# Pacing the side work of a gather-driven kernel: one generator counts more of its steps, two others get other stretches

## The chip, the cores and the metric

The kernel runs on one core of a Trainium2 chip. The metric is the device time of one execution in microseconds (us), from launch to the end of the last instruction. A core has five engines that run side by side, each in the order its instructions were written: TensorE (PE in the profile, PEld for its weight loads), VectorE (DVE), ScalarE (ACT), GpSimd (POOL) and SyncE (SP), which here only issues DMAs.

## What is computed

Four layers with residuals on four images of 256 channels and 64 x 64 pixels, all in float32. Each layer first normalizes its input over groups of channels (`_gn`).

```python
x = x + deformable(_gn(x))   # 1x1 conv, 3x3 depthwise -> offsets and masks, bilinear sampling
                             # at 9 points in 4 groups, projection, squeeze-excite, feed-forward
x = x + linear(_gn(x))       # qkv (1x1), 5x5 depthwise of q, k, v, linear attention, projection
x = x + binary(_gn(x))       # 3x3 convolution with binarized weights
x = x + pooled(_gn(x))       # attention of 4096 pixels over 1024 max-pooled ones, projection
...
# linear: per group of 8 channels, over (qkv, its depthwise convolution)
vk = einsum('bhdn,bhen->bhde', v, k)
out = einsum('bhde,bhen->bhdn', vk, q) / (einsum('bhe,bhen->bhn', k.sum(-1), q) + EPS)
```

## The kernel before

The work is written by Python generators. Each is one piece of one layer for one image, writes a few instructions and yields a cost, a number that stands for the time of what it has just written. A sampling of one image (`sample`) sets the beat: it has 16 blocks of 18 rounds, 288 rounds in all. A round issues four indirect gathers on POOL (L596), of 128 rows each, into one of seven buffers `g`, and then 16 small matmuls (L603) that weigh and add the rows into the accumulator `acc`. Every two rounds ACT copies the accumulator (`at`, L608), PE turns it (`dp`, L613) and ACT copies it on (`dT`, L623). Every 18 rounds PE projects the block (`po`, L636), and the result goes to memory as `x2`.

`beside(steps, number, *works)` writes the other generators in between. Each work has a total cost and a stretch from `lo` to `hi`, as shares of the sampling. After each round a work writes steps as long as what it has spent is below its total times its share of the stretch. Whatever is left when `hi` is reached is written at once. PE, DVE, ACT and POOL keep the written order (`manual_schedule`), so the pacing is the order of each engine's queue.

Beside sampling n run, for n from 1 on: feed-forward of image n-1 (`feed`, matmuls L739 and L749, cost 328), linear attention of image n-1 (`linear`), and, for n of 2 and 3, convolution and pooled attention of image n-2 in one generator (`second`, cost 568; matmuls L1085, then L1142, then per tile L1185, L1197, L1203). Sampling 0 has the first convolutions of the next images beside it. After sampling 3 the rest is written without a sampling: image 3's feed-forward, its linear attention with image 2's `second`, then image 3's `second`. There `self.alone` is true.

Linear attention makes its rows of q, k, v with matmuls (L821), pads them and runs 24 depthwise chains of 25 taps on DVE (L178, in `depthwise`); after three taps it calls `step(3.9)`. `step` takes one item from the list `later`, if there is one, and runs it. The last third of the chains are those of q. After each pair of them (there are four) `output` puts its work into `later` by way of `staged`, as 15 items: denominators (L921) and their reciprocal (L926), twice four heads (`rden`, L934, and `ot`, L938) and twice two projections (L943) with their relu (L947) and sum (L951). The items of one output are taken during the next pair; those of the last output when the chains are over, in the loop `while later` at the end of `layer1`. An item taken in a step adds nothing to the cost that the step yields.

Of the kernel before, what the change touches and what calls it, by code (L numbers as in the profile page):

```python
# [38 lines left out]

CONVOLVE, OFFSETS, BINARY = NB * 9 + 26, 60, 62  # L40
FEED = NB * 40 + 8
LINEAR, LAST = 938, 624
STEPS = 900
CONV, SECOND = NB * 22.5 + 11, 568
EPS_BN = 1e-5
EPS_GN = 1e-5
# [25 lines left out]
class Net:  # L72
# [684 lines left out]
    def layer1(self, n, st, st2):  # L757
# [3 lines left out]
        with tc.tile_pool(name=f"la{n}", bufs=1, side="right") as sp, \  # L761
# [13 lines left out]
            later, count, aside = [], 0, None  # L775
            alone = self.alone
            room = lambda bufs, more=1: bufs + more * alone

            def step(cost, chains=False):


                nonlocal count
                count += chains
                if later and (not alone or count % 2 or not chains):
                    later.pop(0)()
                if chains:
                    if count % 8 == 6 if alone else count in LEADS:
                        next(made, None)
                    if count % 2 and aside:
                        next(aside, None)  # L790
                return cost
# [3 lines left out]
            def staged(items):  # L795


                for i in range(len(items) + max(map(len, items)) - 1):
                    now = [it[i - k] for k, it in enumerate(items) if 0 <= i - k < len(it)]
                    later.append(lambda now=now: [f() for f in now])  # L800

            sums = self.ps1.tile([P, 2, 2, P], F32, name="vk", tag="vk")
            ks = [sp.tile([P, 2, NB], F32, name=f"ks{t}") for t in range(2)]
# [38 lines left out]
            def aggregate(pd, i, name, done, relu=True, **more):  # L842

                acc = self.ps1.tile([P, 16, W], F32, name="agg", tag="agg")
                out = bp.tile([P, 16, W], F32, name=name, tag="ag", bufs=3)
                yield from self.depthwise(acc, pd, self.w5[:, i], 5, 16, W, 0, bias=self.b5[:, i:i + 1],
                                          step=lambda cost: step(cost, True), out=out)
                end(out, done, relu, **more)
# [12 lines left out]
            def outer(t, kind, kv, vv, first, last):  # L861
# [28 lines left out]
                if alone:  # L890
                    staged([(partial(turned, cs), partial(copied, i), partial(added, i)) for i, cs in enumerate(at)])
                else:
                    later.extend(partial(both, i) for i in range(len(at) + 1))
# [16 lines left out]
            def output(c, qp, aq):  # L910
# [48 lines left out]
                if alone:  # L959
                    order = [heads[0, j] for j in range(4)] + [heads[1, 0], outs[0, 0], heads[1, 1], outs[0, 1], heads[1, 2], heads[1, 3]]  # L960
                    staged([(dens, inverse), none, none] + order + [none, outs[1, 0], outs[1, 1]])
                else:
                    joined = lambda *fs: [f() for f in fs]
                    items = [(partial(joined, dens, inverse),), none]
                    for h in range(2):
                        items += [(partial(joined, *heads[h, j]),) for j in range(4)]
                        items += [(partial(joined, *outs[h, m][:2]), outs[h, m][2]) for m in range(KT)]
                    staged(items)
# [25 lines left out]
            if alone:  # L994
                for _ in range(8):
                    next(made)
                    yield step(0.5)
                    yield step(0.5)
# [22 lines left out]
                    yield from aggregate(*args, **more)  # L1021
                    number += 1
            while later:
                yield step(2 if alone else 4)


    def layer2(self, n, st, st3, side="left"):
# [190 lines left out]
    def run(self):  # L1218
        self.setup()
        tile = lambda name, shape: self.cp.tile(shape, F32, name=name)  # L1220
        ssum = [tile(f"ssum{n}", [P, KT, NBLK]) for n in range(N)]
        st = {i: [tile(f"st{i}{n}", [P, KT, NB, 6]) for n in range(2)] for i in (1, 2, 3)}

        feed = lambda n: self.feedforward(n, ssum[n], st[1][n % 2])
        linear = lambda n: self.layer1(n, st[1][n % 2], st[2][n % 2])

        conv = lambda n, side="left": self.layer2(n, st[2][n % 2], st[3][n % 2], side)
        pooled = lambda n, wide=False: self.layer3(n, st[3][n % 2], wide)

        def second(n):  # L1230
            yield from conv(n)
            yield from pooled(n)

        def beside(steps, number, *works):


            spent, open_ = [0] * len(works), set(range(len(works)))

            def advance(share):
                for j in sorted(open_):  # L1240
                    work, total, lo, hi = works[j]
                    while j in open_ and lo <= share and spent[j] < total * (share - lo) / (hi - lo) or share >= hi:
                        cost = next(work, None)
                        if cost is None:
                            open_.discard(j)
                        if not cost:
                            break
                        spent[j] += cost

            for i, _ in enumerate(steps, 1):  # L1250
                advance(i / number)
            while any(works[j][3] <= 1 for j in open_):
                advance(1)

        rounds = NBLK * BR
        E = mybir.EngineType
        ordered = lambda: self.tc.manual_schedule(engines={E.PE, E.DVE, E.Activation, E.Pool})
        behind = lambda n: [(feed(n), FEED, 0, 0.2), (linear(n), LINEAR, 0.2, 1)]
        with self.tc.tile_pool(name="gather", bufs=2, side="left") as self.gp, \
                self.tc.tile_pool(name="samp", bufs=2, side="left") as self.sp:  # L1260
            with self.tc.tile_pool(name="pw", bufs=1, side="right") as wp, \
                    self.tc.tile_pool(name="pa", bufs=1, side="right") as sp, \
                    self.tc.tile_pool(name="pb", bufs=2, side="right") as bp:
                w = self.weights(wp)

                pads, used = [], []  # L1270
                convolved = (y for i in range(1, N) for y in self.convolve(i, w, sp, bp, pads, used))
                shifted = lambda first, last: (self.shifts(first, last, w["mw"], bp, pads, used), (last - first) * OFFSETS)
                beside(range(64), 64, (self.convolve(0, w, sp, bp, pads, used), CONVOLVE, 0, 1), (*shifted(0, 1), 0.3, 1))
                with ordered():
                    beside(self.sample(0, ssum[0]), rounds, (convolved, (N - 1) * CONVOLVE, 0, 0.96), (*shifted(1, N * NCH), 0, 1))
            with ordered():
                beside(self.sample(1, ssum[1]), rounds, (self.binarise(), BINARY, 0, 0.2), *behind(0))
                for n in range(2, N):
                    beside(self.sample(n, ssum[n]), rounds, *behind(n - 1), (second(n - 2), SECOND, 0.2, 0.9))
        self.idle, self.alone, self.spare = cycle(["acc", "dp"]), True, True  # L1280
        rest = second(N - 2)
        with ordered():
            beside(range(STEPS), STEPS, (feed(N - 1), FEED, 0, 0.27), (linear(N - 1), LAST, 0.27, 1), (rest, SECOND, 0.27, 1.05))
        self.spare = False
        beside(range(STEPS), STEPS, (conv(N - 1, "right"), CONV, 0, 1), (rest, 150, 0, 1))

        self.banks = cycle(["mm", "mm", "mm", "vk"])
        for _ in pooled(N - 1, True):
            pass
# [94 lines left out]
```

## Time and profile before

| | |
|---|---|
| median of 3 runs | 7713.78 us (7711.9 to 7732.44) |
| the profiled execution | 8695.07 us, span 8693.3 us, mean granted TensorE clock 0.803 |
| gathers of sampling 0, first to last | 137 to 1908 us |
| sampling 1 | 1909 to 3615 us |
| sampling 2 | 3616 to 5405 us |
| sampling 3 | 5405 to 7191 us |
| first matmul L739 of image 3's feed-forward | 7234 us |

The profile comes from one execution under the profiler, which takes longer than the others; all durations and waits are from it. A group of instructions is named by its line, engine and operation, then output tile and input tiles. After the bar stand its busy time in us, the mean of one in ns, and the idle time of its engine just before it, with what ended that idle time. "Remote" is an event whose source the profile does not tell.

### The profile page before, as it was taken

Reading aid. Unit: us, or ns where it says so; the run is one execution under the profiler, and the core shown is the slowest. Engines: PE = TensorE matmul, PEld = TensorE weight load, DVE = VectorE, ACT = ScalarE, POOL = GpSimd, SP = SyncE. Lnnn points to the kernel's source line nnn. Section 1 sums busy time; section 2 is a strip of 40 time slices with the busy share of each in tenths; the row PEclk is TensorE's granted clock in tenths of the full one; section 3 lists DMA queues with packets and bytes.
Section 4 is the critical chain, followed back from the end, with each engine's and each line's share of the span. In section 5 each row is a group of like instructions: output and inputs, shape, how many; then the busy total and the mean of one; then the engine's idle time right before and its main releaser. Section 6 shows DMA issues by size and latency. Waiting matters only on the chain.

```text
span 8693.3 us, 99761 instructions
## 1 busy us (share of the span) xinstructions
PE 5880.0 (68%) x35776; PEld 3498.6 (40%) x35776; DVE 4817.7 (55%) x6045; ACT 3541.0 (41%) x10767; POOL 4934.7 (57%) x4870
## 2 busy tenths in 40 slices
PE   4454554448744446688876676888766778986899
PEld 2232222224323222234644443345544333664476
DVE  5344442443366667324776675228766762699833
ACT  2333333234444433334445443444454442456414
POOL 2666666466666666666666556666655560476410
PEclk7676766669866667799988887999878879998899
DMA  6454554444533334444543344445433342220131
GB/s 172 129 160 123 145 149 118 114 143 148 158 107 106 110 109 126 137 127 138 142 133 111 111 116 138 146 135 142 141 105 111 112 118 96 74 72 29 44 97 54
DMA packets 744383, 1031.75 MB, mean 119 GB/s; under 512 B 354128, under 2 KB 459984, under 8 KB 742352
## 3 DMA queue, kind: packets, MB, share of 16 engines
q0 software_dynamic: 221184, 604.27, 24.4%
q1 hardware_dynamic: 522704, 421.10, 16.4%
q8 instruction: 283, 4.64, 0.2%
q14 instruction: 212, 1.74, 0.1%
HBM read 856.39 MB, written 168.61 MB: 118 GB/s over the span
## 4 chain that ended last, share of the span: by engine, by line
PE 43%; another core or an unknown queue 17%; DVE 17%; ACT 13%; issue 8%; DMA 1%; POOL 0%; SPq 0%; ACTq 0%; DVEq 0%; POOLq 0%
DVE agg L178 10%; PE acc L603 6%; PE ps L739 5%; PE ps L749 5%; ACT wm L588 5%; PE ps L1085 4%; PE ps L821 3%; PE ps L943 2%; PE ps L1203 2%; PE s L1185 2%; PE po L636 2%; ACT dT L623 2%; ACT at L608 1%; PE rden L934 1%
## 5 line engine op out<-in xcount | busy, mean ns | idle before, releaser
L596 POOL DMA_INDIRECT g<-tab,sl x4608 | 4399.0, 955 | 2790.8 <-issue 1179.7
L178 DVE SCALAR_TENSOR_TENSOR agg<-pad,vec,agg 128x1024 f32<-128x1024 f32 x2280 | 2934.5, 1287 | 63.9
L603 PE MATMUL acc<-g,wm 128*32 128x128 f32 x18432 | 1012.4, 336 | 2022.6 <-ACT at L608 1471.8
L603 PEld LDWEIGHTS acc<-g,wm 128*32 128x32 f32 x18432 | 557.7, 129 | 2524.7 <-ACT at L608 1683.4
L588 ACT ACTIVATE wm<-sl,con 128x48 f32<-128x48 f32 x6144 | 1490.1, 366 | 26.0 <-remote 12.6
L1085 PE MATMUL ps<-xd,w 128*128 128x256 f32 x3072 | 741.0, 392 | 37.6 <-issue 30.1
L623 ACT COPY dT<-dp 64x128 f32<-64x128 f32 x1152 | 297.2, 258 | 985.8 <-remote 524.3
L1085 PEld LDWEIGHTS ps<-xd,w 128*128 128x128 f32 x3072 | 587.3, 196 | 159.0 <-issue 79.0
L739 PE MATMUL ps<-x2f,f 128*128 128x512 f32 x1024 | 502.3, 639 | 10.2 <-issue 5.1
L608 ACT COPY at<-acc 128x256 f32<-128x256 f32 x576 | 214.5, 372 | 712.8 <-remote 607.4
L821 PE MATMUL ps<-xr,qw 128*128 128x512 f32 x768 | 463.5, 733 | 21.8 <-issue 8.5
L724 DVE SCALAR_TENSOR_TENSOR hm<-ps,vec,lk 128x512 f32<-128x512 f32 x256 | 190.6, 750 | 502.4 <-ACT lk L741 375.2
L749 PE MATMUL ps<-hm,f 128*128 128x512 f32 x1024 | 463.6, 601 | 0.0
L741 ACT ACTIVATE lk<-ps,low 128x512 f32<-128x512 f32 x256 | 174.0, 687 | 514.7 <-PE ps L739 413.2
L636 PE MATMUL po<-dT,ow 128*128 128x288 f32 x1024 | 336.7, 477 | 56.5 <-issue 13.8
L875 ACT COPY kt<-pt 128x512 f32<-128x512 f32 x256 | 149.5, 585 | 544.8 <-remote 246.8
L1036 POOL TENSOR_TENSOR xd<-xp 128x640 f32<-128x640 f32 x64 | 79.8, 1275 | 497.3 <-DMA xq<-x 280.3
L1203 PE MATMUL ps<-gt,pT 128*128 128x129 f32 x2048 | 316.5, 315 | 47.1 <-ACT pT L1199 32.9
L613 PE MATMUL dp<-ident,at 128*128 128x128 f32 x1152 | 285.5, 336 | 77.1 <-ACT dT L623 53.4
L1203 PEld LDWEIGHTS ps<-gt,pT 128*128 128x128 f32 x2048 | 297.2, 226 | 98.8 <-ACT pT L1199 45.0
L1185 PE MATMUL s<-ph,th 128*128 128x512 f32 x512 | 289.2, 677 | 42.9 <-DVE ot L938 9.2
L739 PEld LDWEIGHTS ps<-x2f,f 128*128 128x128 f32 x1024 | 199.2, 203 | 253.3 <-issue 238.5
(243 smaller groups left out, 7710.6 us busy)
## 6 DMA issues: line engine op xcount, KB each, us to landing
g<-tab,sl POOLq DMA_INDIRECT x4608
x<-x SPq DMA_DIRECT2D x128, 512.0 KB
xr<-x SPq DMA_DIRECT2D x96, 512.0 KB
tab<-xo SPq DMA_DIRECT2D x192, 128.0 KB
x<-in_x SPq DMA_DIRECT2D x32, 512.0 KB
y<-yc SPq DMA_DIRECT2D x32, 512.0 KB
yb<-y SPq DMA_DIRECT2D x64, 256.0 KB
x<-yb SPq DMA_DIRECT2D x64, 256.0 KB
```

What stands on the lines that cost most here:

```text
L178: nc.vector.scalar_tensor_tensor(to, s, wt, acc, ALU.mult, ALU.add)
L588: nc.scalar.activation(wm[:, :, :, o], blocks[b][:, r:r + WR, G:], AF.Copy, scale=self.con("own")[:, o:o + 1])
L596: nc.gpsimd.indirect_dma_start(out=g[:, i, :], out_offset=None, in_=table, in_offset=bass.IndirectOffsetOnAxis(ap=sl.bitcast(I32)[:, r, i: ...
L603: nc.tensor.matmul(acc[32 * i:32 * i + 32, :], wm[:, r4, 4 * i + 2 * x:4 * i + 2 * x + 2, :], g[:, i, x * P:(x + 1) * P], start=x == 0, st ...
L623: nc.scalar.copy(dT[b][hs, :, r:r + UR], dp[u][hs, :, :, s, :].rearrange("p v g o -> p g v o"))
L636: nc.tensor.matmul(po[m][:, 0:BR * OB], self.ow[:, k, m * P:(m + 1) * P], dT[b][:, k].rearrange("p r o -> p (r o)"), start=k == 0, stop=k ...
L739: nc.tensor.matmul(ps, f1[:, k, m * P:(m + 1) * P], x2[:, k], start=k == 0, stop=k == KT - 1)
L749: nc.tensor.matmul(ps, f2[:, k, m * P:(m + 1) * P], hm[:, k], start=k == 0, stop=k == 4 * KT - 1)
L821: nc.tensor.matmul(ps, qw[:, k, m * P:(m + 1) * P], x[:, k], start=k == 0, stop=k == KT - 1)
L1085: nc.tensor.matmul(ps[:, e], w[:, k, t, 2 * half + e, m * P:(m + 1) * P], v[:, 2 * half + e, k, t:t + 8], start=i % 6 == 0, stop=i % 6 == 5)
L1185: nc.tensor.matmul(s[i], tv[:, 4 * b + j], ph[:, i * 512:(i + 1) * 512], start=True, stop=True)
L1203: nc.tensor.matmul(ps[:, 0:P + 1], pT[:, m], gt[:, m], start=m == 0, stop=m == 7)
```

## The change

Items that `staged` puts into `later` carry a cost of 1.1, and `step` adds it to what it yields when it has taken such an item, unless linear attention runs without a sampling. In the closing loop a step costs 1 instead of 4 beside a sampling. The total `LINEAR` becomes 956. Feed-forward runs over 0 to 0.22 of a sampling instead of 0 to 0.2, linear attention over 0.22 to 1 instead of 0.2 to 1, and convolution with pooled attention over 0.22 to 1 instead of 0.2 to 0.9.

```diff
-LINEAR, LAST = 938, 624
-STEPS = 900
+LINEAR, LAST = 956, 624
+STEPS, BEGUN = 900, 0.22
...
                 if later and (not alone or count % 2 or not chains):
-                    later.pop(0)()
+                    todo = later.pop(0)
+                    todo()
+                    cost += 0 if alone else getattr(todo, "cost", 0)
...
                     later.append(lambda now=now: [f() for f in now])
+                    later[-1].cost = 1.1
...
             while later:
-                yield step(2 if alone else 4)
+                yield step(2 if alone else 1)
...
-        behind = lambda n: [(feed(n), FEED, 0, 0.2), (linear(n), LINEAR, 0.2, 1)]
+        behind = lambda n: [(feed(n), FEED, 0, BEGUN), (linear(n), LINEAR, BEGUN, 1)]
...
-                    beside(self.sample(n, ssum[n]), rounds, *behind(n - 1), (second(n - 2), SECOND, 0.2, 0.9))
+                    beside(self.sample(n, ssum[n]), rounds, *behind(n - 1), (second(n - 2), SECOND, BEGUN, 1))
```

## The prediction

> **What bounds the kernel now.** I read the page first, its 40 slices and then its costliest groups. GpSimd's indirect gathers fill the span until 7190 us; there each has a fixed price.
>
> ```profile
> span 8693.3 us, 99761 instructions
> ...
> L596 POOL DMA_INDIRECT g<-tab,sl x4608 | 4399.0, 955 | 2790.8 <-issue 1179.7
> ```
>
> A gather takes 0.955 us and 0.256 us of issue (1179.7/4608), plus waits. Four gathers are a round, 288 rounds a sampling. So I cut samplings 1, 2 and 3 into stretches of 8 rounds (32 gathers) at the gathers' starts in the timeline, and asked for the busy time of each engine in each. The columns are stretch, length, then busy time of PE, PEld, DVE, ACT and POOL, the granted clock, DMA share and GB/s. The first row is from sampling 1 (linear attention alone), the rest from sampling 2.
>
> ```profile
> 3569.20:3615.25 46.05, 31.64 (x160) 13.49 (x159) 8.70 (x14) 14.17 (x52) 30.33 (x32) 0.70 0.38 112
> sum 1706.62, PE 1018.62 PEld 533.92 DVE 978.68 ACT 681.00 POOL 1100.51; mean PE 28.30 PEld 14.83 DVE 27.19 ACT 18.92 POOL 30.57
> ...
> 4892.17:4945.05 52.88, 35.03 (x262) 23.12 (x262) 35.61 (x47) 25.39 (x82) 30.36 (x33) 0.87 0.41 122
> 4945.05:4991.59 46.54, 29.17 (x210) 18.30 (x209) 33.33 (x37) 23.52 (x72) 30.34 (x32) 0.82 0.38 103
> ...
> 5044.31:5098.03 53.72, 43.66 (x238) 23.64 (x238) 41.48 (x51) 23.91 (x77) 30.32 (x32) 0.80 0.43 124
> 5098.03:5156.51 58.48, 43.02 (x273) 24.89 (x272) 41.36 (x46) 26.12 (x77) 30.77 (x33) 0.88 0.34 98
> ...
> 5312.41:5358.63 46.22, 27.34 (x186) 12.25 (x179) 25.80 (x24) 17.31 (x63) 30.37 (x32) 0.75 0.45 141
> 5358.63:5404.74 46.11, 28.79 (x159) 12.12 (x160) 8.60 (x14) 14.16 (x52) 30.43 (x32) 0.73 0.38 113
> sum 1789.18, PE 1331.60 PEld 795.05 DVE 1061.93 ACT 795.65 POOL 1096.30; mean PE 36.99 PEld 22.08 DVE 29.50 ACT 22.10 POOL 30.45
> ```
>
> POOL's busy time is 30.4 us in all of them, so the length tells what the side work costs the gathers. Undisturbed stretches take 46.0 to 46.5 us; I take 46.5 as the floor, 1674 us a sampling. Over it lie 33 us in sampling 1, 115 in sampling 2, 112 in sampling 3 (1786.08): 260 us. The last 16 rounds (46.2 and 46.1) have no excess: convolution and pooled attention are done there, the DVE chains run dry (25.8, 8.6 us). The worst stretch, 58.5 us, lies just before.
>
> What holds a gather back is in the groups of two windows, about rounds 230 to 259 of sampling 2 and 200 to 230 of sampling 1:
>
> ```profile
> L596 POOL DMA_INDIRECT g<-tab,sl x115 | 109.5, 952 | 84.9 <-PE acc L603 50.5 <-issue 28.0 <-PE pt L1197 2.0
> L596 POOL DMA_INDIRECT g<-tab,sl x115 | 109.0, 948 | 58.1 <-issue 30.4 <-remote 19.4 <-PE po L636 4.0
> ```
>
> POOL waits for L603, the matmuls that empty one of the seven buffers `g`. The waits of the first window say why PE is late (who, for whom: total, times, longest):
>
> ```profile
> ACT pr L947 <- PE ps L943: 40.0, 8, 7.8
> PEld acc L603 <- ACT at L608: 24.3, 5, 8.5
> PE acc L603 <- ACT at L608: 20.5, 4, 8.3
> ACT pe L1191 <- DVE mx L1187: 17.8, 6, 5.9
> ```
>
> ACT waits up to 7.8 us for an output's projection; the copy L608 that frees the accumulator is queued behind; L603 waits for that copy. All engines run in written order, so the excess comes from how much side work is written between two rounds.
>
> **What the Trainium skill says.** "TensorE: Matmul & The Clock Gate", section Part 1 (the clock gate): PE runs at half rate until it has been busy a few microseconds. The trace agrees: granted clock 0.70 to 0.88 above, and eight matmuls L943 take 3.70 us warm (7199.93) and 6.30 us at 7183.95. I use both as ends. The same page, on the array's architecture, calls ACT's and DVE's queues strict FIFO; the 40.0 us wait and the 20.5 us behind it agree. No page prices a pacing.
>
> **The change, part by part.** No instruction, DMA or wait is added or removed; SP's and POOL's queues hold the same work, and only the side work's place among the rounds moves. Costs are counted from the yields.
>
> *Totals.* Linear attention spends 14 (normalization, fold) + 18 (six steps of 3 to fill) + 24 chains x 9 steps x 3.9 = 842.4, and 16 left-over items x 4 = 64: 938.4. After: 16 x 1 for those, plus 60 staged items x 1.1 = 66: 956.4. Both fit their constants; nothing is left to drain.
>
> *Rates per round.* Feed-forward 328/57.6 = 5.69, then 328/63.4 = 5.18 (-9%). Linear 4.07, then 956/224.6 = 4.26. Convolution and pooled attention 568/201.6 = 2.82, then 568/224.6 = 2.53 (-10%). A pair of chains takes 17.2 rounds; after, 16.5 without items (+4.5% work per round), but 20.4 with an output's fifteen items (70.2 + 16.5 at 4.26; -15%).
>
> *Places.* Pooled attention's tiles: rounds 147 to 259, then 163 to 288. First output's items: from 221, then 219. Last output's items, alone: rounds 272 to 288 before, 280 to 288 after.
>
> *How length follows PE's work.* Among sampling 2's pooled stretches, PE busy of 29 to 31 us goes with 46.5 to 47.7 us of length, 35 to 37 with 52.5 to 53.8, and 43 with 54 to 58. I take 1 us of length per us of PE's work beyond 29.
>
> *Pooled attention before outputs.* Rounds 152 to 224: PE busy averages 32.8 us in sampling 2, 21.9 in sampling 1, so pooled attention is 10.9, linear about 11 (the rounds' own matmuls are some 11: 0.65 us each round, the turns and L636). Change: -1.1 + 0.5 = -0.6 us. Excess 4.2 us per stretch (38 us over 9, mean of both samplings) becomes 3.6; over 56 rounds 25 us.
>
> *With outputs.* Rounds 224 to 272: 39.4 and 29.5 us. Change: -15% of 18.5 and -10% of 9.9, -3.8 us. Excess 6.6 us falls towards 2.8; I take 3.3, over 61 rounds 25 us. Together 50 us against 76 (sampling 2) and 81 (sampling 3): -26 and -31.
>
> *The new tail.* Fifteen items in 8 rounds: eight heads at 1.4 us (1.12 and a switch), four projections at 3.70, denominators 2.5 (the 16 matmuls L921 take 1.94 to 3.25), the reciprocal before the first head 3.35: 32 us warm, 43 cold. Rounds' own 13, pooled attention in 19 cost units about 10. Sum 55 to 66 us against 46: +9 to +20, I take +15 in samplings 2 and 3, +5 in sampling 1, which has no pooled attention. The seven buffers hide part; after sampling 3 nothing does: feed-forward's first matmul (7234.28) waits behind this tail and L636. A pooled store that comes late on SP holds the x2 store behind it; that is within this term.
>
> *Feed-forward.* PE busy some 42 us per stretch, near its limit; excess of the first 64 rounds 22, 18 and 11 us. 9% less per round cuts a third: -6, -6, -4. Bounds 0 and -30 in all.
>
> *Convolution*, excess 15 us: a tenth thinner, over more rounds, beside chains 4.5% denser: 0, within ±8; DVE (37 to 41 us there) covers the denser chains. *The stage after the samplings* (1500 us): its branch adds nothing to a step's cost; 0.
>
> Sum: -1 (sampling 1), -17, -20 = **-38 us** of the profiled execution's 8695.07 (span 8693.3): 0.9956. The shown median, 7713.78, is 0.887 of that execution; I scale by the ratio: **7680 us**. Undisturbed gathers may be quicker without the profiler, and then PE decides more.
>
> **Rivals.** *Slower: the tail becomes the bound.* Outputs and pooled attention overlap for 69 rounds instead of 38. If the excess belongs to the overlap, not to its density, 61 rounds at 6.6 and 56 at 4.2 per 8 cost 79 us, no gain; cold PE and ACT behind L943 make the tail +29, +29 and +10. With feed-forward's -16 that is +52 us: 7760. For it: the worst stretches are that overlap. Against it: length follows PE's work among neighbouring stretches. It decides from the point where the tails cost 26 us more (0.3%) than the stretches before them and feed-forward give.
>
> *No change.* Every pooled block costs a fixed stall (76/8 = 9.5 us) at any rate; tails +35, feed-forward -16: +19 us, 7731. The alternation 52.88, 46.54 speaks against it.
>
> *Larger gain.* If each us taken from PE frees twice that (its chain through ACT and DVE shortens too), pooled stretches fall to 25 us: -50 each; with feed-forward -16 and tails +35, -81: 7642.
>
> *It doesn't do what it says:* an item without the attribute costs 0, and the end drains early or late; the count above says otherwise. Worth some 5 us.
>
> **Numbers.** My case 0.43 and the larger gain 0.15: faster 0.58. No change 0.20. Slower 0.22. Within 0.3% (23 us) is about what a measurement of this kernel can tell from no change. Range 7630 to 7745: the gain's doubled slope below, half of the slower case above.
>
> **What would show it.** Samplings 2 and 3 (1789, 1786 us between first and last gather) near 1772 and 1766; POOL's wait for L603 in rounds 230 to 259 falling from 50 to about 30 us; L1185 running to the end of each sampling; rounds 280 to 288 longer than 46 us; the stage after unchanged. Wrong if samplings 2 and 3 keep their length, or if last gather to first L739 grows by over 30 us from 43.

## The result, and the profile after

The changed kernel takes **7638.01 us** (median of 4, 7631.35 to 7642.47) against 7715.94 us for the kernel before on the same chip: a ratio of **0.9893, 95% interval 0.9878 to 0.9909**. That is 78 us, 2.3 times the 34 us between the forecast of 7680 and the median of 7713.78 that the forecast started from.

One fact has to come ahead of the profile. The profile that the prediction read is of an execution of 8695.07 us, while all times shown with it lie near 7714. The prediction took the gap for the cost of profiling. It is not: a profiled execution of the same kernel before, on chip 13 (run f0_before below), took 7718.16 us, with a span of 7716.4. The chips that this kernel met fall into two kinds. On the first (here **kind A**) the kernel before takes 7712 to 7732 us, on the second (**kind B**) 8649 to 8793. The measurement above is of kind A, the profile of before is of kind B. No chip showed both kinds (chip 8 was met twice, each time as B), but the record does not say which chips the first times and the first profile came from. That the kind belongs to the chip, and not to some passing condition, is therefore likely and not shown. The profile after, which is of kind A, is set beside f0_before, not beside the page that the prediction shows.

From the pages of f0_before and then of the changed kernel (line, engine, operation, tiles, count; busy us, mean ns; idle us before it and what ended it):

```profile
span 7716.4 us, 99761 instructions
...
L596 POOL DMA_INDIRECT g<-tab,sl x4608 | 4404.1, 956 | 1832.8 <-issue 1259.8
```

```profile
span 7629.6 us, 99735 instructions
...
L596 POOL DMA_INDIRECT g<-tab,sl x4608 | 4401.1, 955 | 1715.8 <-issue 1271.0
```

The gathers are as many and as long as before; POOL idles 117 us less ahead of them. (The line numbers of code after the edits are higher by 3: L943 is now L946, L1185 is L1188.)

Sampling 2 in five stretches (rounds 0-80 left out: 80-144 convolution, 144-216 pooled attention, 216-272 pooled attention with outputs, 272-288 the end, then rounds 0-64 of sampling 3). The columns are stretch, length, busy time of PE, PEld, DVE, ACT and POOL, granted clock, DMA share, GB/s. First f0_before, then the changed kernel:

```profile
3496.27:3841.17 344.90, 287.65 (x2168) 211.92 (x2160) 301.56 (x360) 172.84 (x575) 246.18 (x257) 0.93 0.56 158
3841.17:4232.06 390.89, 273.56 (x2127) 184.59 (x2120) 314.34 (x360) 217.86 (x693) 272.82 (x288) 0.85 0.45 129
4232.06:4573.46 341.40, 259.04 (x1659) 142.99 (x1658) 276.34 (x303) 163.34 (x519) 212.45 (x224) 0.83 0.45 133
4573.46:4653.98 80.52, 58.40 (x406) 26.76 (x406) 36.53 (x41) 33.70 (x122) 61.33 (x64) 0.80 0.51 151
4654.28:4991.28 337.00, 297.60 (x1604) 138.50 (x1596) 76.10 (x121) 155.85 (x517) 242.50 (x256) 0.97 0.52 153
```

```profile
3480.40:3806.06 325.66, 286.64 (x2157) 216.18 (x2146) 308.69 (x345) 167.89 (x564) 246.37 (x256) 0.95 0.56 158
3806.06:4180.51 374.45, 264.57 (x2050) 174.95 (x2049) 323.87 (x382) 208.91 (x675) 273.18 (x289) 0.84 0.48 142
4180.51:4484.44 303.93, 234.17 (x1604) 132.30 (x1603) 245.81 (x274) 156.23 (x499) 213.16 (x225) 0.88 0.48 138
4484.44:4571.96 87.52, 69.06 (x456) 39.04 (x456) 64.00 (x73) 45.19 (x150) 60.87 (x64) 0.87 0.46 139
4572.27:4935.15 362.88, 312.49 (x1714) 146.37 (x1714) 80.94 (x129) 161.65 (x529) 241.98 (x256) 0.95 0.53 158
```

Three stretches got shorter (345 to 326, 391 to 374, 341 to 304), two got longer (81 to 88, 337 to 363). POOL's busy time is the same in each row to within 1 us, so lengths again tell what the side work costs the gathers. The third row loses 37 us of length with 25 us of PE's work (259.0 to 234.2). Where that work went is in PE's groups of that stretch, f0_before first:

```profile
L603 PE MATMUL acc<-g,wm 128*32 128x128 f32 x928 | 45.7, 325 | 59.3 <-ACT at L608 59.3
L943 PE MATMUL ps<-ot,pw 128*128 128x512 f32 x81 | 39.5, 629 | 0.0
```

```profile
L603 PE MATMUL acc<-g,wm 128*32 128x128 f32 x896 | 40.0, 301 | 37.2 <-ACT at L608 37.2
L946 PE MATMUL ps<-ot,pw 128*128 128x512 f32 x64 | 31.4, 635 | 0.0
```

There are 17 matmuls of projections fewer here. They now run later: behind the last gather of the sampling 32 of them are left, where there were 8. L603, which empties the gather buffers, waits 22 us less for ACT's copy of the accumulator (59.3 to 37.2). POOL's groups show the same from its side; its wait for L603 falls from 71.9 to 27.4 us:

```profile
L596 POOL DMA_INDIRECT g<-tab,sl x224 | 212.4, 948 | 131.6 <-PE acc L603 71.9 <-issue 57.0 <-DMA g<-tab,sl 2.1
```

```profile
L596 POOL DMA_INDIRECT g<-tab,sl x225 | 214.1, 952 | 91.1 <-issue 57.5 <-PE acc L603 27.4 <-DMA g<-tab,sl 3.4
```

The work comes back after the last gather of a sampling. PE's timeline after the last gather of sampling 3 (start us, length us, instruction), in the changed kernel, where that gather ends at 6118.20, and then in f0_before, where it ends at 6238.21:

```profile
6147.40 3.70 PE L946 MATMUL ps<-ot,pw 128*128 128x512 f32 x8
6150.94 1.95 PE L1206 MATMUL ps<-gt,pT 128*128 128x129 f32 x16
...
6179.72 2.93 PE L739 MATMUL ps<-x2f,f 128*128 128x512 f32 x3 [1.75 <-ACT f L714]
```

```profile
6238.11 3.70 PE L943 MATMUL ps<-ot,pw 128*128 128x512 f32 x8
...
6266.78 3.78 PE L739 MATMUL ps<-x2f,f 128*128 128x512 f32 x4 [1.75 <-ACT f L714]
```

Feed-forward's first matmul L739 came 28.6 us after the end of the last gather; now it comes 61.5 us after it, behind projections and pooled attention's tiles in turn (+33). From that matmul to the end both take 1450 us (1449.6, 1449.9).

### The profile page after: what moved, and what is told of

The parts are those of the page before. It is cut to its first block, busy times and chain, and to the rows that moved or that the text cites. A ratio compares the mean times of both kernels' runs of the same rounds, so it can differ in the third digit from the quotient of the medians.

```text
span 7629.6 us, 99735 instructions
## 1 busy us (share of the span) xinstructions
PE 5886.1 (77%) x35776; PEld 3454.3 (45%) x35776; DVE 4810.4 (63%) x6045; ACT 3530.1 (46%) x10767; POOL 4936.3 (65%) x4870
## 3 DMA queue, kind: packets, MB, share of 16 engines
q0 software_dynamic: 221184, 604.27, 27.4%
## 5 line engine op out<-in xcount | busy, mean ns | idle before, releaser
L603 PE MATMUL acc<-g,wm 128*32 128x128 f32 x18432 | 1264.0, 321 | 1161.9 <-ACT at L608 670.8
L603 PEld LDWEIGHTS acc<-g,wm 128*32 128x32 f32 x18432 | 622.1, 121 | 1836.7 <-ACT at L608 888.3
L1088 PE MATMUL ps<-xd,w 128*128 128x256 f32 x3072 | 721.6, 386 | 8.0 <-DVE x L1072 3.5
L739 PE MATMUL ps<-x2f,f 128*128 128x512 f32 x1024 | 489.8, 625 | 4.0 <-ACT f L714 4.0
L608 ACT COPY at<-acc 128x256 f32<-128x256 f32 x576 | 214.1, 372 | 423.1 <-PE acc L603 411.2
L741 ACT ACTIVATE lk<-ps,low 128x512 f32<-128x512 f32 x256 | 175.9, 687 | 500.5 <-PE ps L739 498.2
L1206 PE MATMUL ps<-gt,pT 128*128 128x129 f32 x2048 | 297.6, 304 | 29.8 <-ACT pT L1202 29.1
L613 PE MATMUL dp<-ident,at 128*128 128x128 f32 x1152 | 265.2, 317 | 65.7 <-ACT dT L623 62.9
L636 PE MATMUL po<-dT,ow 128*128 128x288 f32 x1024 | 297.3, 438 | 21.8 <-ACT dT L631 8.9
L1188 PE MATMUL s<-ph,th 128*128 128x512 f32 x512 | 281.6, 663 | 32.9 <-DVE ot L941 11.0
L200 POOL TENSOR_TENSOR ak<-ak,m 128x1024 f32<-128x1024 f32 x96 | 227.6, 2371 | 117.2 <-ACT m L196 112.8
L727 DVE TENSOR_TENSOR xyf<-xyf,ps 128x512 f32<-128x512 f32 x64 | 44.0, 687 | 402.1 <-PE ps L749 389.3
```

The costliest lines, as they stand in the source:

```text
L603: nc.tensor.matmul(acc[32 * i:32 * i + 32, :], wm[:, r4, 4 * i + 2 * x:4 * i + 2 * x + 2, :], g[:, i, x * P:(x + 1) * P], start=x == 0, st ...
L636: nc.tensor.matmul(po[m][:, 0:BR * OB], self.ow[:, k, m * P:(m + 1) * P], dT[b][:, k].rearrange("p r o -> p (r o)"), start=k == 0, stop=k ...
L739: nc.tensor.matmul(ps, f1[:, k, m * P:(m + 1) * P], x2[:, k], start=k == 0, stop=k == KT - 1)
L1088: nc.tensor.matmul(ps[:, e], w[:, k, t, 2 * half + e, m * P:(m + 1) * P], v[:, 2 * half + e, k, t:t + 8], start=i % 6 == 0, stop=i % 6 == 5)
L1188: nc.tensor.matmul(s[i], tv[:, 4 * b + j], ph[:, i * 512:(i + 1) * 512], start=True, stop=True)
L1206: nc.tensor.matmul(ps[:, 0:P + 1], pT[:, m], gt[:, m], start=m == 0, stop=m == 7)
```

## The experiments

All ratios are to the kernel before on the same chip. Chips 7, 8, 10, 0, 12 and 15 turned out to be of kind B; only the first measurement and chip 13 were of kind A. So the parts of the change were separated on kind B alone.

### Which execution was profiled: e0_before, f0_before

Both are the kernel before, unchanged, profiled once each. The first theory was that the profiled execution was disturbed, or slowed by the profiler.

> The kernel before, unchanged, profiled again, because its first profiled execution took 8695 us against a median of 7714. Theory (the first execution was disturbed at the gathers): span near 7712 us, eight undisturbed rounds take about 40 us as in the kernel after, not 46.5; over that floor (1440 us a sampling) the excess is larger than the 33, 115 and 112 us that the prediction read. Rival (the profiler always costs this kernel 1000 us and the change took that cost away): span near 8690 us again.

Measured on chip 8: 8691.73 us, and 8685.22 us (median of 50) for its other executions there. So neither a bad execution nor the profiler is the reason: on that chip the kernel always takes that long. The theory fell.

> The kernel before, profiled again. If this chip is one with 5.0 us rounds (time near 7715), the trace shows in the same regime as the changed kernel's first profile where its 78 us were: theory F (feed-forward at 5.69 per round is over PE's reach when a round takes 5.0): 30 to 45 us over the changed kernel in the first 64 rounds of samplings 1 to 3; theory D (DVE over-full where outputs meet pooled attention): 40 us or more in rounds 220 to 272 of samplings 2 and 3; theory S (stretch of pooled attention): in rounds 147 to 220. If the chip is one with 5.8 us rounds: 8660 to 8780 again, and the excess as in the first profile.

Measured on chip 13: 7718.16 us, beside 7715.21. The same program, profiled, is 11% shorter. Its page against that of before, in section 4 (the chain that ended last, as shares of the span), f0_before first:

```profile
PE 37%; DVE 19%; POOL 7%; issue 6%; ACT 6%; DMA 4%; SPq 0%; DVEq 0%; POOLq 0%; ACTq 0%
```

```profile
PE 43%; another core or an unknown queue 17%; DVE 17%; ACT 13%; issue 8%; DMA 1%; POOL 0%; SPq 0%; ACTq 0%; DVEq 0%; POOLq 0%
```

On kind B 17% of the chain hangs on events of unknown source. Two groups say where, again f0_before first:

```profile
L608 ACT COPY at<-acc 128x256 f32<-128x256 f32 x576 | 214.4, 372 | 378.7 <-PE acc L603 362.7 <-issue 4.0
```

```profile
L608 ACT COPY at<-acc 128x256 f32<-128x256 f32 x576 | 214.5, 372 | 712.8 <-remote 607.4 <-PE acc L603 54.7 <-PE ps L749 11.5
```

The copy takes 372 ns on both, but on kind B its start is mostly set by a "remote" event. The timelines show one hand-off from PE to ACT each; f0_before:

```profile
2447.28 3.78 PE L821 MATMUL ps<-xr,qw 128*128 128x512 f32 x4
...
2451.10 0.78 ACT L829 ACTIVATE v<-ps,g_add,vec 128x512 f32<-128x512 f32 x1 [8.27 <-PE ps L821]
```

and the kernel before on kind B:

```profile
2997.65 0.69 PE L613 MATMUL dp<-ident,at 128*128 128x128 f32 x2
...
3004.97 0.53 ACT L623 COPY dT<-dp 64x128 f32<-64x128 f32 x2 [5.54 <-remote]
```

On A ACT starts 0.04 us after the matmul's modelled end, on B 6.6 us after it, and it was idle for 5.5 of these. Over sampling 0 the copy L608 starts 0.09 us after the last L603 of its two rounds on A and 6.2 us after it on B (medians). L603 waits 750.5 us for L608 on A (its group on the page of f0_before) and 1471.8 on B. So PE falls behind: in sampling 0 a round's first L603 starts 1.9 us after the start of the round's last gather on A, but 30.0 us after it on B (medians), though a gather's packets end about 2.4 us after its start on both. PE runs behind the gathers through the chain L603, L608, L603, and eight rounds take 46.5 us instead of 40.0. That POOL waits for buffers which this chain frees late fits, but is in part argued: between 500 and 1500 us of sampling 0 on B, POOL's waits end on L603 for 47.2 us and on remote events for 117.7. Why B hands over late is not settled; the records do not show it.

### One part at a time: counting, feed-forward, convolution and pooled attention

Theory A was that counting carries most of the gain, theory B that the longer stretches do. Both take the parts to add up. The rival: each part acts through what it collides with, and the parts do not add.

e1_count, q1_count and r1_count are counting alone, on three chips:

```diff
-LINEAR, LAST = 938, 624
+LINEAR, LAST = 956, 624
...
+                    cost += 0 if alone else getattr(todo, "cost", 0)
...
+                    later[-1].cost = 1.1
...
-                yield step(2 if alone else 4)
+                yield step(2 if alone else 1)
```

> Only the counting: items cost 1.1, the closing loop costs 1, the total is 956; all stretches as before (0.2, 0.2 to 0.9). Theory A (outputs that nobody counted overload the rounds they share with pooled attention): most of the gain, -40 us or more of the -78. Theory B (the stretches carry the gain): within 10 us of before. The tail is then denser, but without pooled attention beside it, so theory B allows up to +10.

> Only the counting, once more, for a chip with 5.0 us rounds (before near 7715). There the stretch with outputs and pooled attention (rounds 216 to 272) gave 37 us in each of samplings 2 and 3. If counting thins it: -15 to -25 us in each, ratio 0.994 to 0.997. If thinning pooled attention alone does it: 0.999 to 1.002. On a 5.8 us chip: 1.000 as before.

> Only the counting, for a chip with 5.0 us rounds (before near 7715), where it has not been seen alone. If counting thins the outputs' stretch (rounds 216 to 272: 37 us each in samplings 2 and 3 for the whole change): -15 to -25 us in each, ratio 0.994 to 0.997. If the later end alone does it: 0.999 to 1.002. On a 5.8 us chip: 0.999 to 1.000 a third time.

Measured: 1.000 [0.9989, 1.0012], 0.9993 [0.998, 1.0006] and 1.0009 [0.9999, 1.0019]. Nothing comes of it, and the stretches say why. In e0_before and e1_count, both on chip 8, rounds 216 to 272 of sampling 2 take (columns as above):

```profile
4948.86:5309.15 360.29, 256.36 (x1622) 141.19 (x1621) 275.84 (x303) 161.33 (x511) 213.16 (x225) 0.83 0.43 128
```

```profile
4957.00:5307.70 350.70, 248.61 (x1593) 139.13 (x1591) 242.81 (x269) 157.87 (x509) 212.72 (x225) 0.83 0.44 130
```

10 us are gained there, and given back at the head of the next sampling: its first 8 rounds go from 49.9 to 59.0 us (sampling 2) and from 55.3 to 60.0 (sampling 3).

e2_feed is feed-forward's longer stretch alone:

```diff
-        behind = lambda n: [(feed(n), FEED, 0, 0.2), (linear(n), LINEAR, 0.2, 1)]
+        behind = lambda n: [(feed(n), FEED, 0, 0.22), (linear(n), LINEAR, 0.22, 1)]
...
-..., (second(n - 2), SECOND, 0.2, 0.9))
+..., (second(n - 2), SECOND, 0.22, 0.9))
```

> Only 0.22 in place of 0.2 for feed-forward's end and the begin of the other two; convolution and pooled attention still end at 0.9, nothing is counted. Theory B1 (with gathers at 1.25 us feed-forward at 5.69 per round is over what PE can take, three times): -25 to -40 us. Theory A: 0 to -10, since convolution and pooled attention get denser by 3%.

Measured: 0.9971 [0.9958, 0.9983], 21 us. It is the only part that gains by itself.

e3_second and q3_second are the later end alone, on two chips:

```diff
-..., (second(n - 2), SECOND, 0.2, 0.9))
+..., (second(n - 2), SECOND, 0.2, 1))
```

> Only the end of convolution and pooled attention from 0.9 to 1 (begin 0.2): 12% thinner. Theory B2 (pooled attention's density is what the rounds can't take): -30 to -50 us. Theory A: within 10 us, since it moves work into the last rounds that already hold the outputs.

> Only the end of convolution and pooled attention at 1 instead of 0.9, once more for a chip with 5.0 us rounds. If thinning it by 11% is what pays there: convolution's rounds -15 and pooled attention's -15 in each of samplings 2 and 3, outputs' -15, less 10 to 30 us for each end: ratio 0.992 to 0.997. If it is counting: 0.999 to 1.003. On a 5.8 us chip: 1.0025 as before.

Measured: 1.0025 [1.0014, 1.0035] and 1.0033 [1.0023, 1.0042]. Alone it loses: the last 16 rounds go from 92 to 101 us in sampling 2 and from 90 to 98 in sampling 3 (chip 8), the first 8 of sampling 3 from 55.3 to 61.6, and the stretch with outputs gets no shorter (360 to 369). So no theory of a single part held: counting was to bring 40 us or more and brought none, the later end 30 to 50 and cost 23 and 26, the longer feed-forward 25 to 40 and brought 21.

Then two parts of the three, and all of them, on chip 10. e4_count_second has e1's and e3's edits, e5_count_feed e1's and e2's, e6_feed_second these lines:

```diff
-        behind = lambda n: [(feed(n), FEED, 0, 0.2), (linear(n), LINEAR, 0.2, 1)]
+        behind = lambda n: [(feed(n), FEED, 0, 0.22), (linear(n), LINEAR, 0.22, 1)]
...
-..., (second(n - 2), SECOND, 0.2, 0.9))
+..., (second(n - 2), SECOND, 0.22, 1))
```

> All of the change but 0.22: feed-forward still ends at 0.2, convolution and pooled attention run from 0.2 to 1, items are counted. If 0.22 carries the gain, this is back near before (ratio 0.998 to 1.002); if counting with the later end carries it, ratio within 0.003 of the changed kernel.

> All of the change but the later end: convolution and pooled attention run from 0.22 to 0.9. If the later end costs time (alone it gave 1.0025 with 46.5 us per eight rounds), this is faster than the changed kernel by 10 to 20 us; if the tail is free and thinning pays, slower by 15 us or more.

> All of the change but the counting. If counting is worth nothing (alone it gave 1.000), equal to the changed kernel within 0.002; if counting only pays together with the later end, because pooled attention then lies beside the last output too, slower than the changed kernel by 15 us or more.

a0_after is the changed kernel itself:

> The changed kernel, unchanged, measured once more beside the kernel before. Theory (the gain depends on how long a gather takes on the chip at hand): on a chip where eight undisturbed rounds take 46.5 us (before: about 8685) the gain is the -38 us of the prediction or less, ratio 0.994 to 1.0; on one where they take 40 us (before: about 7714) it is -78 us again, ratio 0.987 to 0.991. Rival (the gain is a matter of written order alone): -78 us on both.

Measured: e4 1.0025 [1.0015, 1.0034], e5 1.0011 [1.0, 1.0023], e6 0.9999 [0.9991, 1.0008], a0 **0.9962 [0.9943, 0.9982]**. Two things follow. On kind B the change brings a third of what it brings on A (27 us here, 39 and 45 in the two pairs below, against 78). And its parts do not add: no pair gains, all three together do. (The single parts were measured on chips 7, 8 and 12, the pairs on chip 10 alone.) Rounds 216 to 272 of sampling 2 show one pair at work, e6_feed_second and then a0_after:

```profile
4950.53:5323.69 373.16, 273.81 (x1629) 151.09 (x1629) 281.42 (x314) 157.99 (x499) 213.14 (x224) 0.81 0.39 115
```

```profile
4964.80:5314.82 350.02, 261.13 (x1603) 144.10 (x1602) 247.53 (x274) 158.58 (x503) 212.19 (x225) 0.80 0.41 120
```

Once pooled attention reaches the end, counting is worth 23 us in this stretch: with it 12.7 us of PE's work and 34 us of DVE's are left for later. e4, which has counting and the later end, still takes 362.7 us there; that is not explained.

### Two suspects for kind B: h0_before, h7_after, d0_before, d7_after

Theory G: on B the gathers are bound by their data transfers, and that hides the change. If so, gathers of half the bytes would bring B's rounds down to A's, and the change up to A's gain. Theory D: DVE is over-full on B; if so, more work on DVE would change what the edits bring. h0_before gathers half of each row and both matmuls read that half (the right neighbours are left out); h7_after is the change with the same:

```diff
-                    out=g[:, i, :], out_offset=None, in_=table,
+                    out=g[:, i, 0:P], out_offset=None, in_=table,
...
-                                     g[:, i, x * P:(x + 1) * P], start=x == 0, stop=x == 1)
+                                     g[:, i, 0:P], start=x == 0, stop=x == 1)
```

> The kernel before, but each gather fetches half a row (128 of 256 floats), and both matmuls of a group read that half; so the right-hand neighbours' samples are left out and replaced by the left-hand ones. POOL's and PE's instructions are the same in number and size. Theory G (on these chips the gathers are bound by the DMA queue, which lags 27 us behind their issue; where the queue keeps up, POOL's 1.25 us per gather is the floor): an undisturbed eight rounds take 40 us, the lag of the first matmul L603 behind the issue of its round falls from 27 us to below 5 in sampling 0, and the time is near 7715 us. Rival (the lag is a fixed latency of a landing, or goes by the number of descriptors): floor stays at 46 us, time within 1% of before.

> The changed kernel with the same halved gathers (right-hand samples left out). Theory G: its distance to the halved kernel before is that of the first measurement, 0.987 to 0.991 (some -78 us), where with whole rows on such a chip it was 0.996. Rival (the -78 us came from something else of that chip): 0.994 to 0.998 again.

Measured: 1.0013 [0.9997, 1.0029] and 0.9961 [0.9949, 0.9972]. Theory G fell: the gathers' queue moves 302 MB instead of 604, and that changes nothing; the number of gathers stayed, so a limit by their number is not tested. The change is worth 0.9961/1.0013 = 0.9948 on the halved gathers. The two profiles are a pair of before and after from one chip of kind B, which serves below.

d0_before adds one DVE reduction of about 0.68 us after every three taps beside a sampling; d7_after is the change with the same:

```diff
+            if k == 5 and not self.alone and (t % 3 == 2 or t == k * k - 1):
+                nc.vector.tensor_reduce(self.zero[:, 128:132], ..., AX.X, ALU.max)
```

> The kernel before with one more DVE instruction after every three taps of linear attention's chains beside the samplings (a maximum over 128x512 zeros, about 0.69 us, result unused): some 0.72 us more of DVE per round. Theory D (why the change gave 0.989 where a round takes 5.0 us and 0.996 where it takes 5.8: DVE needs, per round with outputs and pooled attention, about 4.0 for taps, 0.9 for an output's items and 0.7 for pooled attention, 5.6 us; that is over 5.0 and under 5.8): with the addition it needs 6.3 us there, over 5.8 also on such a chip, so this is slower than before by 20 to 60 us, with the loss in rounds 220 to 259 of samplings 2 and 3. Rival L (the rounds wait on PE and ACT alone): within 10 us of before.

> The changed kernel with the same additional DVE instructions (an unused maximum after every three taps). Theory D: its DVE need stays under 5.8 us per round (5.6 without outputs, 5.4 with), so its distance to the loaded kernel before grows from 0.996 to 0.987 to 0.991. Rival L: 0.995 to 0.997 again. If this chip has rounds of 5.0 us (before near 7715), both are DVE-bound for most of the samplings, and the ratio shrinks towards 1 under theory D.

Measured: 1.0044 [1.0025, 1.0063] and 0.9999 [0.9987, 1.001]; the change is worth 0.9999/1.0044 = 0.9955 here. In d0_before theory D had its way: it asked for 20 to 60 us more, and 40 came, though no plain profile of this chip shows in which rounds. It fell with d7_after, where it asked for 0.987 to 0.991: on kind B the change brings no more when DVE has more to do. On kind A this was not tested.

### An earlier end: i1_end97, i2_end97

If the tails are paid because pooled attention's last tiles meet the last output's items, the change with `second` ending at 0.97 of the sampling keeps most of the thinning and loses the meeting:

```diff
-..., (second(n - 2), SECOND, BEGUN, 1))
+..., (second(n - 2), SECOND, BEGUN, 0.97))
```

> The changed kernel with convolution and pooled attention ending at 0.97 instead of 1, just before the last output's items are alone (round 280). The changed kernel lost 25 us at the head of sampling 3 and 33 us after the last gather to that overlap. If the overlap is the cause: these two fall to below 10 us, pooled attention 4% denser gives back 5 to 12 us in each sampling, so 15 to 40 us quicker than the changed kernel: ratio to before 0.984 to 0.987 on a 5.0 us chip, 0.992 to 0.995 on a 5.8 us chip. If the closing items alone are too dense: like the changed kernel, 0.989 and 0.996.

> The changed kernel with convolution and pooled attention ending at 0.97, once more. On a 5.0 us chip (before near 7715) the overlap at the end cost the changed kernel 25 us at the head of sampling 3 and 33 us after the last gather; if the earlier end removes it there too: ratio 0.984 to 0.987; if not, 0.989. On a 5.8 us chip, where the first look at it gave 0.9957 and shorter ends (390 against 407 us for the first 64 rounds of sampling 3, 1506 against 1521 us after the last gather): 0.993 to 0.996.

Measured on chips 7 and 8: 0.9957 [0.994, 0.9974] and 0.9956 [0.9945, 0.9968]. The first lies outside the 0.992 to 0.995 that was hoped for, and neither can be told from the change itself (0.9962). The tails shrank only in part. Against e0_before on chip 8 the last 16 rounds together with the next sampling's first 8 grew by 8 us after sampling 2, where h7_after grew by 18 against h0_before. From the start of the last gather to the first L739 it is 59.9 us (49.9 before), where h7_after has 63.1 (48.3). (The time from the last gather to the end, 1505.6 against 1507.8, hides this, since the last stage, which the edit doesn't touch, was 12 us shorter.) And the stretches with outputs gained less: 9 and 10 us, against 15 and 19 in h7_after. It wasn't run on kind A, so no version here is shown to beat the changed kernel.

## Why the prediction was right, and where it failed

Its terms against two pairs of profiles, in us for samplings 1, 2 and 3. A tail is the last 16 rounds together with the next sampling's first 8; after sampling 3 it is the way to the first L739. Feed-forward is rounds 8 to 64. Kind B is h7_after against h0_before, both on chip 0; kind A is the changed kernel against f0_before, which were taken apart, f0_before on chip 13.

| term | predicted | kind B | kind A |
|---|---|---|---|
| feed-forward | -6, -6, -4 | -4, -13, +2 | -14, -9, +1 |
| rounds 64-80 | not priced | -2, +2, -2 | 0, +6, +4 |
| convolution, 80-144 | 0 | 0, -3, 0 | 0, -19, -18 |
| pooled attention and outputs, 144-272 | 0, -26, -31 | -7, -30, -36 | -1, -54, -56 |
| tail | +5, +15, +15 | +4, +18, +20 | 0, +32, +40 |

Sampling 0 and the last stage, which the change doesn't touch, differ by +20 and +12 us between the two profiles of kind B, and by +2 and 0 on kind A. So a single term of the B column means little below some 10 us; their sum of -51 us agrees with the ratio 0.9948 (-45 us). The sum of the A column is -89 us (the two spans differ by 87, the medians by 78).

**Right: the mechanism, and on kind B the sum.** Gathers are held back by L603, L603 by ACT's copy, and that by how thickly side work is written. Making it thinner moved POOL's wait as foretold: in rounds 230 to 259 of sampling 2 from 50 to about 30 us in the prediction, from 46.1 to 17.0 measured on A, from 46.9 to 16.1 in the pair of kind B. Pooled attention's matmul L1188 now runs in the last 16 rounds (16 times, none in f0_before), and the last stage is unchanged. On chips of the kind that the profile came from the sum held: -38 us of 8695 is 0.9956, and 0.9962, 0.9948 and 0.9955 were measured on three of them (the last two with altered gathers and with more work on DVE). Part of that is luck. The prediction let the stretches with outputs shrink because PE's work leaves them; in the pair of kind B PE's busy time in rounds 216 to 272 fell by only 6.8 and 0.4 us, while the lengths fell by 15 and 19.

**Wrong: the step "I scale by the ratio".** The prediction saw 8695 beside 7714, called the difference the profiler's, and carried stretches that were read on kind B over to the times of kind A. The factor itself took only 4 us off (38 to 34); what failed is that the terms have other sizes there, -89 us in sum and not -34. Kind A is not kind B with a shorter clock. Busy times are equal (a gather 956 and 955 ns, L608 372 ns on both); what differs is waiting. The floor of 46.5 us for 8 rounds goes with B's late hand-off, and the profile gave a hint of it: 32 gathers of 0.955 + 0.256 us are 38.8 us, so that 7.7 us in each undisturbed stretch were waits that the prediction left unasked. On A the floor is 40.0 us (320.0 for rounds 80 to 144 of sampling 1), and POOL's own busy and issue time is 39.3 of it. Over that floor lie 28, 143 and 144 us in samplings 1 to 3, not 33, 115 and 112. The pool to draw from was bigger, by 55 us, than the one that was priced.

**Wrong on A: three terms.** *Pooled attention and outputs* were put at -26 and -31 and measured -54 and -56. The price "1 us of length per us of PE's work" measured 37/25 = 1.5 for rounds 216 to 272 and 16/9 = 1.8 for rounds 144 to 216. It had been read from some of the stretches; others of the same sampling speak against it (29.8 us of PE's work with 49.8 us of length, 35.2 with 49.5), and a straight line through all stretches of rounds 144 to 272 in samplings 2 and 3 of that profile has a slope of 0.6. So neighbouring stretches did not tell what a change would free.

*Convolution*, put at 0, within 8, measured -19 and -18 in samplings 2 and 3. PE's work in these rounds stayed (287.7, 286.6), but it is not the same work. Convolution's last matmul (L1085) is written at round 125 before and at 139 after, and pooled attention's first matmuls (L1142) at rounds 130 to 144 before and 144 to 160 after. Rounds 128 to 144 of sampling 2, f0_before first:

```profile
3750.28:3795.48 45.20, 24.99 (x206) 17.96 (x206) 37.40 (x60) 15.70 (x56) 30.27 (x33) 0.71 0.51 155
3795.48:3841.17 45.69, 35.75 (x294) 21.89 (x293) 36.49 (x42) 29.60 (x96) 30.88 (x33) 0.99 0.57 170
```

```profile
3723.82:3766.07 42.25, 36.66 (x286) 28.42 (x287) 31.93 (x32) 21.62 (x75) 31.22 (x32) 0.89 0.45 134
3766.07:3806.06 39.99, 38.12 (x283) 28.21 (x282) 39.11 (x45) 22.94 (x80) 30.23 (x32) 1.00 0.54 158
```

That is 9 of the 19 us, and the next 16 rounds, which took this work over, did not get longer (89.6 to 86.0). The other 10 us or so lie in convolution itself (rounds 80 to 128: 254.0 to 243.4). Over rounds 80 to 144 nearly all of the gain is POOL's wait for L603, which falls from 24.7 to 3.4 us:

```profile
L596 POOL DMA_INDIRECT g<-tab,sl x257 | 247.3, 962 | 99.0 <-issue 69.4 <-PE acc L603 24.7 <-DMA g<-tab,sl 3.7
```

```profile
L596 POOL DMA_INDIRECT g<-tab,sl x256 | 246.4, 962 | 79.3 <-issue 70.1 <-DMA g<-tab,sl 4.0 <-PE acc L603 3.4
```

So the mechanism that the prediction priced in pooled attention acted here too, where it put it at nothing. Why thinning by a tenth frees that much in rounds 80 to 128 is open.

*The tail* was put at +15 and measured +32 and +40. One of the prediction's own signs of being wrong thereby came on A: the way from the last gather to the first L739 grew by 33 us.

**The rivals.** The larger gain (slope 2, 7642 us) is where the time landed, and its -50 for pooled attention in each sampling was close. That its total fits is luck all the same: it had +35 for the tails and nothing for convolution, where A shows +72 and -38. The slower rival was right on the tails' place and, for samplings 2 and 3, on their price: +29, +29 and +10, where A shows +32, +40 and, for sampling 1, 0. The likeliest case took its +15 from a sum of 55 to 66 us against 46; against A's floor of 40 the same sum gives +15 to +26. The rival's cold end needs a slow PE (the Trainium skill, "TensorE: Matmul & The Clock Gate", Part 1), but eight matmuls of the projections take the warm 3.70 us in the timeline above, so the rest is waiting in turns between outputs and tiles. The rival failed in its other half, that thinning gains nothing. On A the stretches with outputs gain 37 + 37 us and the tails take 72 back: that part of the change only moves work. What is left, some 85 us, lies where no output is written: feed-forward (-22, with +10 after it), rounds 80 to 144 (-38) and pooled attention ahead of the outputs (-35). That these come from the later end of `second` together with the later start is argued from the rates, not shown: no run on kind A has it alone, and on kind B it loses alone.

Open are what makes kind B hand over late, why convolution itself gains as much as it does on A, and how much counting alone or the later end alone is worth there.

## What to carry to other kernels

Before costing anything, set the profiled execution's own time beside the median: a gap of 13% is to be explained, not scaled away, and a floor that exceeds busy time plus issue is itself a wait. When side work is spread over more rounds, price first what it will meet at the end of its stretch: here that end came just before the next stage, and nothing hid it. When a change moves the borders between stages, compare like work with like work before naming the stage that gained. And test the parts of a pacing change together as well as alone, for here three parts that brought 0, -0.3% and +0.3% alone, and nothing or a loss in pairs, brought -0.4% together (all on kind B).

## What was not expected of the hardware

The same program takes 7716 us on some chips and 8685 to 8765 us on others (medians), with busy times that differ by some 1% or less on each engine. On the slower kind ACT takes up the result of a matmul up to several us late. For ACT's L741 after the last L739 that it needs, the 95th percentile of the gap, beside the samplings, is 0.10 us in both profiles of kind A and 3.9 to 5.8 us in five profiles of kind B. For image 3's feed-forward, which has no sampling beside it, it is 0.04 us on both kinds, and the whole last stage takes 1449.6 us on A and 1459.0 on B in the kernel before. So nearly all of the difference between the kinds lies where the gathers run. The mean granted clock is lower on kind B too (0.80 against 0.84), but eight warm matmuls L943 take 3.70 us on both kinds. Halving the bytes of 4608 gathers, from 1 KB rows to 512 bytes, changed the time by 1.0013 [0.9997, 1.0029] on kind B.
